# A residual stage of a scan kernel: three quarters of the first pair's output are written to DRAM by rows and copied on later

## The chip, the cores and the metric

The kernel runs on one core of a Trainium2 chip. The time is the device time of one execution in microseconds (us); of several runs the median is given. TensorE (PE) does the matrix products, VectorE (DVE), ScalarE (ACT) and GpSimd (POOL) the elementwise work, and 16 DMA engines move data between DRAM and the on-chip memory (SBUF). In this kernel DMAs are issued from two queues: that of SyncE (SP) and that of ScalarE (ACT).

## The reference

The input x has 32 images, 48 channels, 64 rows, 128 columns, in float32. Two layers are applied, each `x = x + scan(groupnorm(x))`, with 16 groups of 3 channels and no affine part. A scan has four passes over the whole picture, each a recurrence with a 5-tap convolution over all 48 channels:

```python
def step(w, b):
    def f(carry, inp):
        nxt = inp + _conv1d(carry, w, b)
        return (nxt, nxt)
    return f
```

Down and up go over the 64 rows (the carry is a row of 128 columns), then right and left over the 128 columns (the carry is a column of 64 rows). The up pass starts from the last row that down made and takes the down results as input; right and left follow in the same way. So the four passes are strictly one after the other: 2 x 63 row steps, then 2 x 127 column steps, and each step needs the one before it.

## The kernel before

**Groups, pairs, phases.** The 32 images are four groups of eight (`GB = 8`). A row phase takes one group through down and up, 126 steps; a column phase takes two groups, a pair, through right and left, 254 steps. Each layer has four row phases and two column phases, and the 12 phases stand in the tuple `PHASES`, numbered 0 to 11: phases 2 and 6 are the column phases of layer 0, phases 10 and 11 those of layer 1, for the first and the second pair. Phase 11 is the last, directly after phase 10.

**A step.** 48 channels are put on 128 partitions together with eight neighbouring columns (in a row phase) or eight row classes (row modulo 8, in a column phase): 384 = 3 x 128, cut as `PIECES` says. A step is nine products of 128 x 128 by 128 x 128 against band-shaped weights (`PRODUCTS`), and three DVE operations that add bias and input (line 650). Each product shows as two matmul instructions, so 18 to a step.

**SBUF.** `arena` has three slots and a stage of four tiles. A slot holds either half the rows of a group or a quarter of the columns (32 of 128) of a pair. A column phase has four quarters and three slots: quarter 0 is written to DRAM in the course of the right scan (`spill_unit`, `spill`), quarter 3 goes into its slot, and quarter 0 is read back in the left scan. `slots(k)` turns the order of the slots around from phase to phase: phase 11's quarter 0 lies in the slot of phase 10's quarter 2, and its quarter 1 in that of quarter 1.

**Through DRAM.** A group's rows are written out by the up scan (`move_rows` with `to_dram`, to `upa` in layer 0 and `upb` in layer 1) in pieces of 32 floats, 128 bytes, and read back by columns with `load_unit`, six units to a quarter (three partition groups for each of the pair's two groups), in pieces of up to 8 KB.

**The residual.** In a column phase of layer 1 each quarter has six units. `load_residual` brings a unit of the layer's input (`mid`) into one of two tiles, by the ACT queue. `add_permuted` adds it to the result on POOL, eight instructions, and puts the sum into one of two output tiles in the order of images and columns. `store_result` writes this to `out`, in pieces of 32 floats, 128 bytes, which is what a row of a quarter has in `out`; half of its DMAs are issued from SP and half from ACT. Quarters are done in the order 3, 2, 1, 0, as the left scan finishes them. In phase 11 the last quarter is done otherwise (`last_loads`, `last_results`).

**Order.** The kernel is one list of instructions, made before the launch. `scans` gives the steps; `at(t, fn, ...)` puts other work into an agenda at step number t, and `catch_up` writes out what is due before each step. `in_order` ties each engine's instructions into the order in which they were written, DMA queues too: an instruction that waits holds up all that stands behind it on its engine. The numbers t are thus places in each engine's order and not times. Semaphores come from the data dependences. All DMAs, from both queues, use eight semaphores in turn.

**The start.** `first_group` writes out the first group's work: loading, group statistics, permuting rows into pieces (POOL), writing them to `xin`, reading them back as rows (`move_rows`), scaling (`scale_rows`, on ACT), and the first load of the second group (`take_in(1, 0, ...)`, on SP).

The lines that the change touches: the weight tiles at 139, `store_result` at 618, the loads at the start of a column phase at 795 to 800, the residual tiles at 823 to 847, the end of `first_group` at 1035 and the agenda behind it, 1038 to 1042.

Of the kernel before, what the change touches and what calls it, by code (L numbers as in the profile page):

```python
# [29 lines left out]
F32 = mybir.dt.float32  # L30
# [3 lines left out]
C = 48  # L34
# [7 lines left out]
GB = 8  # L42
E8 = 8
FULL = 128
NG = E8 * C // FULL
NQ = 4
# [45 lines left out]
def kernel(  # L92
# [11 lines left out]
    NH = H // E8  # L104
    KQ = NK // NQ
    WQ = W // NQ
# [3 lines left out]
    UNIT = NH * LINE  # L110
# [5 lines left out]
    CHANNEL = H * W * GB  # L116
# [5 lines left out]
    dram = ctx.enter_context(tc.tile_pool(name="dram", bufs=1, space=bass.MemoryType.DRAM))  # L122
# [10 lines left out]
    def const(shape, name):  # L133
        return cpool.tile(shape, F32, tag=name, name=name)
# [1 line left out]
    arena = const([FULL, 3 * SLOT + 4 * UNIT], "arena")  # L136
    slot = [arena[:, i * SLOT : (i + 1) * SLOT] for i in range(3)]
    stage = arena[:, 3 * SLOT :].rearrange("p (i n) -> p i n", i=4)
    wt = {k: const([FULL, NG, NG * FULL], f"w{k}") for k in ("down0", "down1", "right", "left")}
    bd = const([FULL, NG, 2, 3], "bd")  # L140
    mask_sb = const([P, P], "mask_sb")
    maskp = const([P, NG, FULL], "maskp")
# [4 lines left out]
    def kept(name):  # L147
# [13 lines left out]
        dram.tile([2 * NG, FULL, UNIT], F32, tag=f"spill{i}", name=f"spill{i}")  # L161
        for i in range(4)
    ]

    def by_row(t, e, h0, h1):

# [14 lines left out]
    def dma(dst, src, queue=None):  # L181
        (queue or nc.sync).dma_start(dst, src)
# [21 lines left out]
    def pieces(o):  # L204
        return [(e, c0, c1, p0) for e, c0, c1, g, p0 in PIECES if g == o]
# [39 lines left out]
    def scaling(key, layer, g, averages, masks):  # L245


        n = len(masks)
        yield from averages(key)
        mean_p, var_p = averages.result  # L250

        def average(ps, rhs):
            for i in range(n):
                nc.tensor.matmul(ps, masks[i], rhs[:, i], start=i == 0, stop=i == n - 1)

        def expand(ps, rhs):
            for o in range(NG):
                nc.tensor.matmul(ps[:, o], maskp[:, o], rhs, start=True, stop=True)

        def small(name):  # L260
            return stat_tile([FULL, NG, GB], name, key)

        ps = ps_stat.tile([FULL, 2 * NG + 2, GB], F32, tag="ps_stat", name=f"ps_{key}")
        average(ps[0:P, 0], mean_p)
        yield
        mean_c = stat_tile([P, GB], "mean_c", key)
        nc.vector.tensor_copy(mean_c, ps[0:P, 0])
        yield
        expand(ps[:, 1 : 1 + NG], mean_c)
        yield  # L270
        mean = small("mean")
        nc.vector.tensor_copy(mean, ps[:, 1 : 1 + NG])
        at = mean if n > 1 else mean_c.unsqueeze(1)
        np_ = FULL if n > 1 else P
        spare = small("dev")
        dev = spare[0:np_, 0:n]
        nc.vector.tensor_tensor(dev, mean_p, at, ALU.subtract)
        nc.vector.tensor_tensor(dev, dev, dev, ALU.mult)
        nc.vector.tensor_tensor(dev, dev, var_p, ALU.add)
        yield  # L280
        average(ps[0:P, 1 + NG], dev)
        yield
        var_c = stat_tile([P, GB], "var_c", key)
        nc.vector.tensor_copy(var_c, ps[0:P, 1 + NG])
        yield
        expand(ps[:, 2 + NG :], var_c)
        yield
        var = small("var")
        nc.vector.tensor_scalar(var, ps[:, 2 + NG :], GN_EPS, None, ALU.add)

        std = small("std")
        nc.scalar.activation(std, var, AF.Sqrt)
        yield
        yield
        r0 = std
        nc.vector.reciprocal(r0, std)
        t0 = spare
        nc.vector.tensor_tensor(t0, var, r0, ALU.mult)
        nc.vector.tensor_tensor(t0, t0, r0, ALU.mult)
        yield  # L300
        nc.vector.tensor_scalar(t0, t0, -0.5, 1.5, ALU.mult, ALU.add)
        scale, offset = (
            stat_pool.tile(
                [FULL, NG, GB], F32, tag=f"{t}{layer}{g}", name=f"{t}{layer}{g}"
            )
            for t in ("scale", "offset")
        )
        nc.vector.tensor_tensor(scale, r0, t0, ALU.mult)
        nc.vector.scalar_tensor_tensor(offset, mean, -1.0, scale, ALU.mult, ALU.mult)
        coeffs[layer, g] = scale, offset  # L310
# [259 lines left out]
    HH = NH // 2  # L570
# [47 lines left out]
    def store_result(k, j, i, perm):  # L618
# [5 lines left out]
        for a in range(HH):  # L624
            for e, c0, c1, p0 in pieces(o):
                to = nc.sync if a < HH // 2 else nc.scalar
                dma(dst[e, r * HH + a, c0:c1], src[p0 : p0 + c1 - c0, a], to)


    def step(key, weights, b_at, src, inp, dst, whole, part):  # L630

# [88 lines left out]
    def at(t, fn, *args):  # L720
        agenda.append((t, len(agenda), fn, args))

    def spread(t, gen, every):


        def go(t):
            if next(gen, "end") != "end":
                at(t + every, go, t + every)
                agenda.sort(key=lambda a: a[:2])

        at(t, go, t)
# [58 lines left out]
    def plan_cols(k, t0, prev):  # L790
        _, layer, pair = PHASES[k]
        n = 2 * NG
        after = prev == "cols"
        for i in range(n):
            if follows(k) and UNITS[i][1] == 1:
                other = nc.scalar
                at(t0 - 13 + i, load_unit, k, 0, i, 2, NH, 0, E8, other)
                at(t0 - 6 + i / n, load_unit, k, 0, i, 1, 2, 0, E8, other)
                at(t0 - 1.5, load_unit, k, 0, i, 0, 1, E8 // 4, E8, other)
                at(t0, load_unit, k, 0, i, 0, 1, 0, E8 // 4, other)  # L800
                at(t0 + 1.5, load_unit, k, 1, i)
            else:
                early = 30 if after else 46 if k == 2 else 70
                at(t0 - early + 2 * i, load_unit, k, 0, i)
                at(t0 + (3 if after else 0.5 if follows(k) else -24 + 2 * i), load_unit, k, 1, i)
            at(t0 + (38 if after else 8) + 2 * i, load_unit, k, 2, i)
            at(t0 + 33 + 2 * i, spill_unit, k, i, False)
            at(t0 + 50 + 2 * i, load_unit, k, 3, i)
        final = k == len(PHASES) - 1
        left = t0 + W - 1  # L810
        end = left + W - 1
        for i in range(n):
            at(left + 64 + 2 * i, spill_unit, k, i, True)
        units = []
        for n_done, j in enumerate((3, 2, 1, 0)):
            every = 4.5
            if j == 0 and PHASES[k + 1 if not final else k][0] == "rows":
                every = 7
            units += [(left + 34 + 32 * n_done + every * i, j, i) for i in range(n)]
        stats = None  # L820
        if layer == 0:
            stats = ResultStatsV(f"r{2 * pair}"), ResultStatsA(f"r{2 * pair + 1}")
        tiles = [stage[:, i] for i in range(4)]
        nats, perms = (tiles, None) if layer == 0 else (tiles[0:2], tiles[2:4])
        ahead = len(nats)

        for u, (t, j, i) in enumerate(units):
            nat = nats[u % ahead]
            o, half = UNITS[i]
            if u < ahead:  # L830
                at(left + 16, load_residual, k, j, i, nat)
            elif not (final and j == 0):
                at(units[u - ahead][0] + (3 if layer == 0 else 4.9), load_residual, k, j, i, nat)
            if layer == 0:
                at(t, add_residual, k, j, i, nat)
                at(t + 4, keep_result, k, j, i)
                unit = quarter(k, j)[:, half, o]
                if half == 0:
                    for b in range(GB):
                        at(t + 5 + b, stats[0].take, j, o, unit, b)  # L840
                else:
                    at(t + 1, stats[1].take, j, o, unit)
            elif not (final and j == 0):
                perm = perms[u % 2]
                at(t, add_permuted, k, j, i, nat, perm, [nc.gpsimd])
                at(t + 5, store_result, k, j, i, perm)
        if layer == 0:
            t = units[-1][0] + 14
            g = 2 * pair
            spread(t, scaling(f"r{g}", 1, g, stats[0], r_masks), 1)  # L850
            spread(t + 20, scaling(f"r{g + 1}", 1, g + 1, stats[1], r_masks), 1)
        if final:
            at(left + 97, last_loads, k)
            at(end + 4, last_results, k)
# [29 lines left out]
    starts = [0]  # L884
# [11 lines left out]
    nats = [wide_nat(3 * SLOT, 4)]  # L896
# [15 lines left out]
    def first_group():  # L912
# [29 lines left out]
        for b in range(2 * GB):  # L942
            i, b = divmod(b, GB)
# [88 lines left out]
        scale_rows(0, 24, 32)  # L1032
        move_rows(0, 32, 48, False)
        scale_rows(0, 32, 40)
        move_rows(0, 48, 56, False)
        take_in(1, 0, nats1[0])

    in_order(first_group)
    at(starts[0] + 10, scale_rows, 0, 40, 48)
    at(starts[0] + 20, move_rows, 0, 56, 64, False)  # L1040
    at(starts[0] + 22, take_in, 1, 16, nats1[1])
    at(starts[0] + 34, scale_rows, 0, 48, 64)

    agenda.sort(key=lambda a: a[:2])
    done = 0
# [65 lines left out]
```

## Time and profile before

| | |
|---|---|
| median of 3 runs | 4545.84 us (4545.33 to 4550.96) |
| the profiled execution | 4548.13 us, span of its instructions 4546.3 us |
| mean granted clock of TensorE | 0.964 |
| busy share of the span: PE, DVE, ACT, POOL | 92%, 48%, 26%, 20% |
| DMA: packets, bytes | 2,124,132, 661.55 MB; 2,010,816 packets under 512 B |
| DMA: mean rate | 146 GB/s |

Phases in the span, by the names of the step tiles: phase 0 from about 140 us, phase 1 from 410, phase 2 (`step_00r`, `step_00l`) from 677, phase 6 (`step_01r`, `step_01l`) from 1995, phase 10 (`step_10r`, `step_10l`) from 3303, phase 11 (`step_11r`, `step_11l`) from 3814 to 4422. A name such as `step_11r` reads: layer 1, pair 1, right; `step_00d` is layer 0, group 0, down. The rest of the span, to 4546, is output.

How to read it: a view of waits gives, for an engine and an operation, what it waited for and for how long, in total, how often, and the longest. Where it names an operation that had long been done, the wait was for another one that ended at the same time, often a DMA. A view by stretches gives the busy time of each engine in a window, the granted clock (1.00 is full speed), the share of the 16 DMA engines and the rate. Every instruction of the residual addition has line 614, every DMA line 182, every product of a step line 641.

### The profile page before, as it was taken

Reading aid. Unit: us, or ns where it says so; the run is one execution under the profiler, and the core shown is the slowest. Engines: PE = TensorE matmul, PEld = TensorE weight load, DVE = VectorE, ACT = ScalarE, POOL = GpSimd, SP = SyncE. Lnnn points to the kernel's source line nnn. Section 1 sums busy time; section 2 is a strip of 40 time slices with the busy share of each in tenths; the row PEclk is TensorE's granted clock in tenths of the full one; section 3 lists DMA queues with packets and bytes.
Section 4 is the critical chain, followed back from the end, with each engine's and each line's share of the span. In section 5 each row is a group of like instructions: output and inputs, shape, how many; then the busy total and the mean of one; then the engine's idle time right before and its main releaser. Section 6 shows DMA issues by size and latency. Waiting matters only on the chain.

```text
span 4546.3 us, 90798 instructions
## 1 busy us (share of the span) xinstructions
PE 4163.2 (92%) x36632; PEld 4132.1 (91%) x36632; DVE 2180.9 (48%) x6594; ACT 1183.5 (26%) x2334; POOL 907.7 (20%) x943
## 2 busy tenths in 40 slices
PE   4889997999999999979999999999999997879990
PEld 2889997999999999979999999999999997869990
DVE  5445443446654444434456654444444443334441
ACT  1553302426776445000025944330000000000000
POOL 4441001314412020000024300000000155500554
PEclk9999998999999999989999999999999998889995
DMA  9989789857989999489038989394790099970799
GB/s 176 176 163 157 114 146 194 202 105 237 221 163 160 162 150 155 75 151 199 6 89 241 204 148 150 48 143 84 117 207 12 18 195 181 200 188 1 148 172 163
DMA packets 2124132, 661.55 MB, mean 146 GB/s; under 512 B 2010816, under 2 KB 2063808, under 8 KB 2092224
## 3 DMA queue, kind: packets, MB, share of 16 engines
q1 hardware_dynamic: 1901312, 573.92, 66.5%
q10 hardware_dynamic: 222400, 81.83, 9.5%
q8 instruction: 288, 4.72, 0.5%
q14 instruction: 132, 1.08, 0.1%
HBM read 378.70 MB, written 277.11 MB: 144 GB/s over the span
## 4 chain that ended last, share of the span: by engine, by line
PE 77%; DMA 15%; SPq 2%; ACT 2%; POOL 1%; ACTq 1%; issue 1%; DVE 0%; POOLq 0%; DVEq 0%
DMA out<-arena 6%; PE step_01r L641 6%; PE step_00r L641 6%; PE step_10r L641 6%; PE step_00l L641 6%; PE step_01l L641 6%; DMA arena<-mid 4%; PE step_11r L641 3%; PE step_00u L641 3%; PE step_11d L641 3%; PE step_02u L641 3%; PE step_11u L641 3%; PE step_10u L641 3%; PE step_13u L641 3%; PE step_13d L641 3%; PE step_12u L641 3%
## 5 line engine op out<-in xcount | busy, mean ns | idle before, releaser
L525 ACT ACTIVATE arena<-arena,offset,scale 128x256 f32<-128x256 f32 (+2 forms) x840 | 594.7, 802 | 449.3 <-DVE arena L650 151.8
L614 POOL TENSOR_TENSOR arena<-arena 128x256 f32<-128x256 f32 x336 | 349.1, 1082 | 973.1 <-DVE arena L650 717.6
L482 POOL COPY arena<-arena 112x256 f32<-112x256 f32 x458 | 270.9, 648 | 764.1 <-DMA arena<-in_x 469.0
L880 ACT COPY arena<-arena 128x256 f32<-128x256 f32 x18 | 10.5, 644 | 1470.9 <-DMA out<-arena 1467.9
L594 POOL TENSOR_TENSOR arena<-arena 128x2048 f32<-128x2048 f32 x48 | 217.7, 4562 | 835.7 <-PE step_01l L641 543.5
L641 PE MATMUL step_11r<-arena,wright 128*128 128x128 f32 x2286 | 267.3, 281 | 85.7 <-DVE arena L650 37.6
L641 PEld LDWEIGHTS step_11r<-arena,wright 128*128 128x128 f32 x2286 | 265.4, 198 | 87.5 <-DVE arena L650 55.8
L416 ACT ACTIVATE junk<-arena 128x256 f32<-128x256 f32 x192 | 129.6, 675 | 699.2 <-POOL arena L594 693.1
L641 PE MATMUL step_01r<-arena,wright 128*128 128x128 f32 x2286 | 258.8, 277 | 29.3 <-DMA arena<-upa 29.3
L641 PEld LDWEIGHTS step_01r<-arena,wright 128*128 128x128 f32 x2286 | 258.4, 194 | 29.7 <-issue 29.5
L641 PE MATMUL step_00r<-arena,wright 128*128 128x128 f32 x2286 | 257.4, 276 | 29.2 <-DMA arena<-upa 29.2
L641 PEld LDWEIGHTS step_00r<-arena,wright 128*128 128x128 f32 x2286 | 257.0, 193 | 29.6 <-issue 29.4
L641 PE MATMUL step_00l<-arena,wleft 128*128 128x128 f32 x2286 | 256.3, 275 | 0.0
L641 PE MATMUL step_10r<-arena,wright 128*128 128x128 f32 x2286 | 256.0, 275 | 0.0
L641 PEld LDWEIGHTS step_10r<-arena,wright 128*128 128x128 f32 x2286 | 255.7, 192 | 0.3
L641 PEld LDWEIGHTS step_00l<-arena,wleft 128*128 128x128 f32 x2286 | 255.7, 192 | 0.0
L641 PE MATMUL step_01l<-arena,wleft 128*128 128x128 f32 x2286 | 255.4, 275 | 0.0
L641 PE MATMUL step_10l<-arena,wleft 128*128 128x128 f32 x2286 | 255.4, 275 | 0.0
L641 PE MATMUL step_11l<-arena,wleft 128*128 128x128 f32 x2286 | 255.4, 275 | 0.0
L641 PEld LDWEIGHTS step_01l<-arena,wleft 128*128 128x128 f32 x2286 | 255.3, 192 | 0.0
L641 PEld LDWEIGHTS step_10l<-arena,wleft 128*128 128x128 f32 x2286 | 255.3, 192 | 0.0
L641 PEld LDWEIGHTS step_11l<-arena,wleft 128*128 128x128 f32 x2286 | 255.3, 192 | 0.0
(173 smaller groups left out, 6989.0 us busy)
## 6 DMA issues: line engine op xcount, KB each, us to landing
xin<-arena SPq DMA_DIRECT2D x96, 384.0 KB, 5.5
arena<-xin SPq DMA_DIRECT2D x96, 384.0 KB, 8.5
mid<-arena SPq DMA_DIRECT2D x96, 384.0 KB, 8.0
arena<-mid SPq DMA_DIRECT2D x192, 192.0 KB, 4.4
upb<-arena SPq DMA_DIRECT2D x192, 192.0 KB, 3.9
arena<-mid ACTq DMA_DIRECT2D x192, 192.0 KB, 4.7
arena<-upb SPq DMA_DIRECT2D x96, 384.0 KB, 10.7
arena<-xin SPq DMA_DIRECT2D x186, 192.0 KB, 4.3
```

The source lines that it names most:

```text
L416: nc.scalar.activation(junk[:, 0:n], view[:, b], AF.Identity, accum_out=self.sum[:, i, j : j + 1])
L482: copy(dst[:, r, q], src[:, r0 + r, q])
L525: nc.scalar.activation(args[0], args[0], AF.Identity, bias=args[2], scale=args[1])
L594: nc.gpsimd.tensor_tensor(unit, unit, nat, ALU.add)
L614: engines[(2 * a + s) % len(engines)].tensor_tensor(dst[:, a, s], res[:, a, s], inp[:, a, s], ALU.add)
L641: nc.tensor.matmul(part(whole(ps[o]), -s), weights[:, i, FULL * (o - NG * s - i + 1) : FULL * (o - NG * s - i + 2)], part(src(i), s), star ...
L880: copy(dst[:, a, s], src[:, a, s])
```

## The change

Five edits:

1. In phase 10, quarters 2, 1 and 0 are no longer written to `out` by `store_result`. `hold_result` writes a unit's sums to a tensor in DRAM, `held[j]`, which has channels, rows, images and the 32 columns of the quarter, in that order; a piece is a row with all its 16 images, 512 floats, 2 KB. One DMA for each entry of `PIECES`, from SP. Quarter 3 goes to `out` as before.
2. In the agenda of phase 11, from step 63 on, 96 DMAs from SP copy from `held` to `out`, each for one image and 24 channels: 1536 pieces of 128 bytes, 192 KB, DRAM to DRAM.
3. In layer 1 the residuals have a third tile, and their loads stand one unit earlier in the order. The tile is the first 2048 of the 2304 columns of `downs`, a tile that joins the weights `down0` and `down1`.
4. In phases 2 and 6, which follow the row phase of their second group, the first quarter's load for that group is cut once more: rows 32 to 63 at 31 steps before the phase, rows 16 to 31 at 13 steps before it, where rows 16 to 63 were.
5. In the first group, rows 56 to 63 are read with rows 48 to 55 in `first_group`, ahead of the first load of the second group, and not at step 20; rows 48 to 55 and 56 to 63 are scaled apart, at steps 26 and 32, and not together at 34.

```diff
@@ -136,7 +136,9 @@
     arena = const([FULL, 3 * SLOT + 4 * UNIT], "arena")
     slot = [arena[:, i * SLOT : (i + 1) * SLOT] for i in range(3)]
     stage = arena[:, 3 * SLOT :].rearrange("p (i n) -> p i n", i=4)
-    wt = {k: const([FULL, NG, NG * FULL], f"w{k}") for k in ("down0", "down1", "right", "left")}
+    wt = {k: const([FULL, NG, NG * FULL], f"w{k}") for k in ("right", "left")}
+    downs = const([FULL, 2, NG, NG * FULL], "downs")
+    wt |= {f"down{i}": downs[:, i] for i in range(2)}
     bd = const([FULL, NG, 2, 3], "bd")
     mask_sb = const([P, P], "mask_sb")
     maskp = const([P, NG, FULL], "maskp")
@@ -161,6 +163,11 @@
         dram.tile([2 * NG, FULL, UNIT], F32, tag=f"spill{i}", name=f"spill{i}")
         for i in range(4)
     ]
+
+    HELD = (2, 1, 0)
+    held = {
+        j: dram.tile([C, 2 * CHANNEL // NQ], F32, tag=f"held{j}", name=f"held{j}") for j in HELD
+    }
 
     def by_row(t, e, h0, h1):
 
@@ -626,6 +633,19 @@
                 to = nc.sync if a < HH // 2 else nc.scalar
                 dma(dst[e, r * HH + a, c0:c1], src[p0 : p0 + c1 - c0, a], to)
 
+    def hold_result(j, i, perm):
+        o, r = divmod(i, 2)
+        n = 2 * GB * WQ
+        dst = held[j].rearrange("c (a e n) -> e c a n", e=E8, n=n)[:, :, r * HH : (r + 1) * HH]
+        for e, c0, c1, p0 in pieces(o):
+            dma(dst[e, c0:c1], perm[p0 : p0 + c1 - c0].rearrange("p (a n) -> p a n", n=n))
+
+    def let_result(j, b, part):
+
+        src = held[j][part].rearrange("c (h b n) -> b (c h) n", b=2 * GB, n=WQ)
+        dst = out[b, part].rearrange("c h w -> (c h) w")
+        dma(dst[:, j * WQ : (j + 1) * WQ], src[b])
+
 
     def step(key, weights, b_at, src, inp, dst, whole, part):
 
@@ -794,7 +814,8 @@
         for i in range(n):
             if follows(k) and UNITS[i][1] == 1:
                 other = nc.scalar
-                at(t0 - 13 + i, load_unit, k, 0, i, 2, NH, 0, E8, other)
+                at(t0 - 31 + i, load_unit, k, 0, i, 4, NH, 0, E8, other)
+                at(t0 - 13 + i, load_unit, k, 0, i, 2, 4, 0, E8, other)
                 at(t0 - 6 + i / n, load_unit, k, 0, i, 1, 2, 0, E8, other)
                 at(t0 - 1.5, load_unit, k, 0, i, 0, 1, E8 // 4, E8, other)
                 at(t0, load_unit, k, 0, i, 0, 1, 0, E8 // 4, other)
@@ -822,6 +843,8 @@
             stats = ResultStatsV(f"r{2 * pair}"), ResultStatsA(f"r{2 * pair + 1}")
         tiles = [stage[:, i] for i in range(4)]
         nats, perms = (tiles, None) if layer == 0 else (tiles[0:2], tiles[2:4])
+        if layer:
+            nats.append(downs.rearrange("p i g n -> p (i g n)")[:, 0:UNIT])
         ahead = len(nats)
 
         for u, (t, j, i) in enumerate(units):
@@ -843,12 +866,20 @@
             elif not (final and j == 0):
                 perm = perms[u % 2]
                 at(t, add_permuted, k, j, i, nat, perm, [nc.gpsimd])
-                at(t + 5, store_result, k, j, i, perm)
+                if final or j not in held:
+                    at(t + 5, store_result, k, j, i, perm)
+                else:
+                    at(t + 5, hold_result, j, i, perm)
         if layer == 0:
             t = units[-1][0] + 14
             g = 2 * pair
             spread(t, scaling(f"r{g}", 1, g, stats[0], r_masks), 1)
             spread(t + 20, scaling(f"r{g + 1}", 1, g + 1, stats[1], r_masks), 1)
+        if layer and not final:
+            for n in range(len(HELD) * 4 * GB):
+                n_done, i = divmod(n, 4 * GB)
+                part = slice(i % 2 * C // 2, (i % 2 + 1) * C // 2)
+                at(end + 63 + 0.95 * n, let_result, HELD[n_done], i // 2, part)
         if final:
             at(left + 97, last_loads, k)
             at(end + 4, last_results, k)
@@ -1032,14 +1063,14 @@
         scale_rows(0, 24, 32)
         move_rows(0, 32, 48, False)
         scale_rows(0, 32, 40)
-        move_rows(0, 48, 56, False)
+        move_rows(0, 48, 64, False)
         take_in(1, 0, nats1[0])
 
     in_order(first_group)
     at(starts[0] + 10, scale_rows, 0, 40, 48)
-    at(starts[0] + 20, move_rows, 0, 56, 64, False)
     at(starts[0] + 22, take_in, 1, 16, nats1[1])
-    at(starts[0] + 34, scale_rows, 0, 48, 64)
+    at(starts[0] + 26, scale_rows, 0, 48, 56)
+    at(starts[0] + 32, scale_rows, 0, 56, 64)
 
     agenda.sort(key=lambda a: a[:2])
     done = 0
```

## The prediction, made before the changed kernel ran

> **What bounds the kernel now.** I read the page first: the product engine is busy 92% of the span, so only the places where it stands still can be won. Then the list of its waits, which gives those places, and then the busy times by stretch, cut at the phase borders.
>
> ```profile
> span 4546.3 us, 90798 instructions
> PE 4163.2 (92%) x36632; PEld 4132.1 (91%) x36632; DVE 2180.9 (48%) x6594; ACT 1183.5 (26%) x2334; POOL 907.7 (20%) x943
> ```
>
> ```profile
> PE rows L970 <- DMA arena<-in_x: 45.0, 1, 45.0
> PE step_11r L641 <- DVE arena L650: 37.6, 4, 18.8
> PE step_00d L641 <- DVE arena L650: 34.8, 3, 19.2
> PE step_11r L641 <- DMA arena<-mid: 32.8, 2, 16.9
> PE step_01r L641 <- DMA arena<-upa: 29.3, 1, 29.3
> PE step_00r L641 <- DMA arena<-upa: 29.2, 1, 29.2
> PE step_11r L641 <- DMA arena<-upb: 15.3, 1, 15.3
> ```
>
> (Engine, operation, what it waited for: total us, times, longest.) The three rows of `step_11r`, the last right scan, hold 37.6+32.8+15.3 = 85.7 us: the largest stop after the start. The two `upa` rows are the starts of the first two column phases.
>
> ```profile
> 3682.00:3814.00 132.00, 132.00 (x1185) 132.00 (x1184) 62.98 (x198) 0.00 (x0) 65.96 (x65) 1.00 0.98 198
> 3814.00:4055.00 241.00, 155.32 (x1288) 153.60 (x1288) 69.31 (x215) 0.00 (x0) 85.93 (x83) 0.80 1.07 214
> 4055.00:4225.00 170.00, 170.00 (x1523) 169.93 (x1523) 81.21 (x254) 0.00 (x0) 0.00 (x0) 1.00 0.05 11
> 4225.00:4420.00 195.00, 195.00 (x1749) 195.00 (x1748) 93.13 (x292) 0.00 (x0) 116.64 (x112) 1.00 0.89 174
> 4420.00:4546.00 126.00, 2.43 (x22) 2.24 (x21) 24.56 (x23) 10.47 (x18) 49.36 (x50) 0.52 1.03 166
> 2670.00:2796.00 126.00, 126.00 (x1132) 126.00 (x1131) 62.82 (x210) 66.28 (x90) 0.00 (x0) 1.00 1.02 147
> ```
>
> (Stretch, length, busy us of PE, its weight loads, DVE, ACT, POOL; then granted clock, DMA share, GB/s.) From 3682 to 4055 the DMA engines are full, and in the second stretch PE works 155 of 241 us, at clock 0.80. It does 1288/18 = 71.6 steps there; a step at full clock is 2.01 us (63 steps of `step_12d` take 126.63), so 144 us would do: 97 us are lost, 86 idle and 11 to the lower clock. Then 170 us follow with the DMA engines at 5%, and then the end, where they are full again and PE has been done since 4422. So the loss is a queue of transfers before an empty stretch.
>
> ```profile
> POOL arena L614 <- DMA arena<-mid: 73.6, 11, 20.5
> POOL arena L614 <- DMA out<-arena: 44.7, 17, 11.4
> POOL arena L614 <- DMA arena<-upb: 29.9, 3, 11.9
> ```
>
> (GpSimd's waits, 3600 to 3980.) The first pair's 24 additions of the residual need 200 us and take 356: 148 us pass waiting for transfers. They free the slots into which the last phase loads its quarters, so each late addition becomes a late load.
>
> **The change, part by part.** *Results held.* 18 of 24 units of phase 10 (quarters 2, 1, 0) no longer go out in 128-byte pieces. Removed are 18 x 13.3 = 240 DMAs, half on SP and half on ACT, with 18 x 8192 = 147,456 pieces. In the stretch 2670 to 2796, where all transfers are 128-byte pieces, 147 GB/s at a share of 1.02 make 14.2 ns a piece and engine: 147,456 x 14.2 / 16 = 131 us of all DMA engines. Added are 60 DMAs on SP alone with 9216 pieces of 2 KB. No such store is in the trace; its packet records have 46 ns for a 1 KB store and 309 for 8 KB, so 77 to 92 ns, I take 85: 49 us. Saved: 82 us of a full queue. ACT then issues only residual loads in these quarters, and no longer stands behind an addition before it can issue the next one. Behind a held store on SP, which waits for POOL's addition, stand the spill and the quarter loads of phase 11, as behind the old stores. All DMAs share eight semaphores in turn, so fewer DMAs also block each other less.
>
> The Trainium skill ("DMA: Bandwidth & Descriptors", "Latency and other measured facts") speaks against this store: row pitches that are large powers of two lose bandwidth, 207 GB/s at 512 KiB and 103 at 4 MiB, and padding restores it. The held tensor has a bare pitch of 128 KiB a channel where the neighbouring tensors are padded; at 103 GB/s the 18.9 MB would cost an estimated 183 us and the gain would turn into a loss. No row here shows that pitch.
>
> *What it buys.* Unless noted, the last right scan would start at 3814 as now. Its quarters are due at 3814, +32 steps = 3878, +64 = 3942, +96 = 4006. From about 3690 the additions can run at their written pace, 9.05 us a unit (4.5 steps) against 8.7 us of POOL work (8 x 1.08): quarter 2 ends near 3750, quarter 1 near 3815 to 3835, quarter 0 near 3880 to 3895. The DMA work due by 3878, by packet records: 16 residual units at 4.25 us (256 packets of 265 ns) = 68, 17 held units at 2.7 = 46, the spilled quarter back 19 (768 at 400), two quarters loaded 29 each (768 at 600): 191 us against 188. So quarters 0 and 1 come about in time. Quarter 2 can load after 3885: spill 15, itself 29, three early residuals of phase 11 13 = 57 us, done near 3942. I leave 10 us of the 97 standing: gain 87, bounds 55 (an over-full queue and two stops left) and 97.
>
> *Passing on.* 96 DMAs on SP, 147,456 pieces, DRAM to DRAM. They wait for held stores alone; SP order puts them behind the quarter-3 loads, so they run from about 3965. Behind them on SP stand only phase 11's outputs, on ACT its residual loads (through the shared semaphores), needed from 3814+255+68 = 4137. Free are 172-13 = 159 us. The trace has no long copy of this kind; its few DRAM-to-DRAM packets (192 B, `taps` from `in_w`) have a median of 15 ns in light traffic, 26 in the crowded start. Bounds: 14.2 (read and write overlap) and 28.4 (they add): 131 to 262 us. I take 15, the nearest row: 138 us, inside 159, cost 0. If the cover goes, every us beyond it delays the full queue of the end, less some 20 us of gaps there. The issues themselves (0.4 to 0.6 us each on SP in the trace, 96 make some 50) fit too.
>
> *Third residual tile.* It removes waits for `mid`, but the two output tiles stay, and waits for stores follow: the end's full queue (0.89, then 1.03) leaves about 15 us. I take 4, bounds 0 and 15. It lies in weight storage last used in phase 9. The merged weight tile costs nothing if dependences go by region, as in `arena`; if not, one weight load (about 15 us) would stop phase 3.
>
> *Rows 32 to 63 loaded earlier at two column starts.* 2/3 of a 2.36 MB load (8 us each time) leaves the last 26 us before the border. DMA share there is 0.52 to 0.72 earlier on and 1.16 later, so it fits. But the chain that ends the stop is store, load, store, load of the last eight rows, and it begins only when row 2 is done. I take 2.5 each of 29: 5, bounds 0 and 16. The ACT queue has nothing else there.
>
> *First group.* Rows 56 to 63 are loaded before the second group's first take-in, not between its two; scaling splits in two. That ends the 19.2 us stop at 227. But the next phase's rows wait for POOL's permutes of the second group, which end at 362.2 by a chain of transfers that PE's pace does not set; the 10 DMAs (10.8 us) now stand before that group instead. Most comes back as a stop at the next border: gain 2, bounds -5 and 10.
>
> Sum: 87+4+5+2 = 98. The profiled execution took 4548.1 (span 4546.3), which makes 4450; the median of the runs is 2.3 lower: 4448.
>
> **Rivals.** *Slower: the copies are dear.* From 3965 a copy at x ns a piece takes 9216x ns. It decides at 159 + 20 + 98 = 277 us, 30 ns a piece; at 45 ns, 415 us, the end comes 138 us after today's: about 4685. For it: read and write both in DRAM, no long row. Against: the 15 ns row, and loads and stores of 128 B each sustain 14.2. *Stops form again:* held stores at 2 x 85 ns add 49 us, or SP's order makes quarters 1 and 2 late; half the gain stays, 4495. *No change:* additions were the pace all along. Against: 24 x 8.7 = 208 us from 3621 end at 3829, not 3977; 4546. *Better:* upper bounds of the small parts, 97+15+16+10: about 4410.
>
> **How the numbers follow.** Forecast 0.60 (its own range 4430 to 4470), stops again 0.20 (4470 to 4530), better 0.06, no change 0.02, slower 0.12 (4556 to 4750). The range 4420 to 4525 leaves out the slower case and the edges. A measurement tells 0.2%, 9 us, from no change; faster 0.86, same 0.02, slower 0.12.
>
> **What would show it.** The `step_11r` rows should fall from 85.7 to under 20 us with clock near 1; waits of POOL for `out` and `mid` should halve. The copies should fill part of the empty stretch and be over before phase 11's first addition; if share 1 runs on into the end and PE-end to span-end grows beyond 125 us, the copy price was wrong. The `upa` waits should be some 27 each, the 19.2 gone, a new wait in `step_01d`.

## The result, and the profile after

The changed kernel takes 4553.43 us (median of 12 runs, 4548.91 to 4558.82) against 4549.59 for the kernel before (12 runs): a ratio of 1.0009, 95% interval 1.0000 to 1.0018. That is no change. The forecast was 4448.

The page of the changed kernel:

```profile
span 4551.0 us, 90606 instructions
PE 4164.5 (92%) x36632; PEld 4133.9 (91%) x36632; DVE 2182.1 (48%) x6594; ACT 1190.0 (26%) x2358; POOL 906.5 (20%) x943
```

PE's waits in it (engine, operation, what it waited for: total us, times, longest):

```profile
PE step_11r L661 <- DVE arena L670: 30.6, 3, 12.1
PE step_10r L661 <- DVE arena L670: 27.0, 2, 18.0
PE step_00r L661 <- DMA arena<-upa: 26.7, 1, 26.7
PE step_11r L661 <- DMA arena<-upb: 26.3, 3, 15.1
PE step_01r L661 <- DMA arena<-upa: 24.5, 1, 24.5
PE step_00d L661 <- DVE arena L670: 20.6, 3, 10.9
PE step_10r L661 <- DMA arena<-upb: 11.5, 1, 11.5
PE step_00u L661 <- DVE arena L670: 9.5, 1, 9.5
```

The last right scan, `step_11r`, waits 56.9 us where it waited 85.7: less, but not the 10 of the forecast. And the right scan of phase 10, `step_10r`, which had no wait before, has two rows, 38.5 us in all. Nothing in the change was meant to touch that scan.

PE's order of time around it (start, length, engine, what ran; in brackets the idle time before):

```profile
3294.06 1.14 PE L661 MATMUL step_10r<-arena,wright 128*128 128x128 f32 x8
3306.68 65.44 PE L661 MATMUL step_10r<-arena,wright 128*128 128x112 f32 x570 [11.48 <-DMA arena<-upb]
3381.15 1.65 PE L661 MATMUL step_10r<-arena,wright 128*128 128x128 f32 x6 [9.04 <-DVE arena L670]
3400.78 192.92 PE L661 MATMUL step_10r<-arena,wright 128*128 128x112 f32 x1702 [17.98 <-DVE arena L670]
...
3848.80 1.06 PE L661 MATMUL step_11r<-arena,wright 128*128 128x128 f32 x8
...
4170.55 255.44 PE L661 MATMUL step_11l<-arena,wleft 128*128 128x128 f32 x2286
```

The starts of the same scans in the kernel before:

```profile
3303.03 256.05 PE L641 MATMUL step_10r<-arena,wright 128*128 128x128 f32 x2286
3814.18 0.61 PE L641 MATMUL step_11r<-arena,wright 128*128 128x128 f32 x4
4167.00 255.43 PE L641 MATMUL step_11l<-arena,wleft 128*128 128x128 f32 x2286
```

With these the books close:

| stretch | before | after | difference |
|---|---|---|---|
| to the start of phase 10 | 3303.0 | 3294.1 | -9.0 |
| phase 10 | 511.2 | 554.7 | +43.6 |
| right scan of phase 11 | 352.8 | 321.8 | -31.1 |
| left scan of phase 11 | 255.4 | 255.4 | 0 |
| from the end of PE to the end | 123.9 | 125.0 | +1.1 |

The sum is +4.6; the spans differ by 4.7 us. So the change did gain 40 us, and a new stop of 44 us took them.

SP's queue, phase 9 and after (the length of a row is the time from its first issue to its last), first two rows of the kernel before, then the changed kernel:

```profile
3086.87 24.62 SPq L182 DMA_DIRECT2D arena<-upb  x20
3190.18 74.05 SPq L182 DMA_DIRECT2D upb<-arena  x50
```

```profile
3078.51 220.98 SPq L189 DMA_DIRECT2D arena<-upb  x20
3299.86 55.19 SPq L189 DMA_DIRECT2D upb<-arena  x50
3355.14 13.86 SPq L189 DMA_DIRECT2D arena<-upb  x14
3369.66 17.02 SPq L189 DMA_DIRECT2D upb<-arena  x10
```

ACT's queue in the changed kernel (3100 to 3660):

```profile
3294.03 3.14 ACTq L189 DMA_DIRECT2D downs<-mid  x7
```

And what SP waited for (3100 to 3420):

```profile
SPq L189 <- DMA downs<-mid: 195.4, 4, 193.9
SPq L189 <- DMA arena<-upb: 13.9, 10, 3.8
```

Issuing the twenty loads of phase 10's first quarters took 25 us before and takes 221 now: seventeen are issued by 3104, the last three not before 3297.8. SP waits 194 us in one piece for a load into `downs`, the third residual tile. ACT issues seven of the eight loads into `downs` at 3294, when phase 9's last products have read the weights there. Behind SP's blocked load stand the 80 stores of phase 9's rows to `upb`, which before began at 3190 and now begin at 3300, and behind these phase 10's loads.

The stretches of the changed kernel (length, busy us of PE, its weight loads, DVE, ACT, POOL, then clock, DMA share, GB/s):

```profile
3660.00:3849.00 189.00, 189.00 (x1695) 189.00 (x1694) 90.23 (x282) 0.00 (x0) 119.98 (x116) 1.00 0.90 206
3849.00:4060.00 211.00, 154.09 (x1298) 152.76 (x1297) 69.78 (x216) 0.00 (x0) 74.61 (x72) 0.85 0.90 227
4060.00:4191.00 131.00, 131.00 (x1175) 130.93 (x1174) 62.65 (x196) 0.00 (x0) 0.00 (x0) 1.00 0.98 155
4426.00:4551.00 125.00, 0.00 (x0) 0.00 (x0) 23.51 (x19) 10.44 (x18) 49.53 (x51) 0.51 1.02 164
```

In the right scan of phase 11 PE still stops, but the DMA engines are no longer full throughout: a share of 0.90 where it was 1.07 (3849 to 4060 in both). The copies from `held` to `out` fill 4060 to 4191, the stretch that was empty, and the part after PE is no longer than it was. GpSimd's waits in the first pair's additions (3640 to 4000), without the wait for the scan itself:

```profile
POOL arena L621 <- DMA held<-arena: 88.9, 4, 40.8
POOL arena L621 <- DMA out<-arena: 31.3, 4, 12.7
POOL arena L621 <- DMA arena<-mid: 11.7, 3, 8.9
```

The waits for residuals (`mid`) fell from 73.6 to 11.7, those for `out` from 44.7 to 31.3, and a new one came, 88.9 us for the held stores: an output tile is not free until its store has landed. In SP's queue one sees why it lands late:

```profile
3798.10 28.57 SPq L189 DMA_DIRECT2D arena<-upb  x10
3827.24 4.36 SPq L189 DMA_DIRECT2D held<-arena  x3
3834.82 18.73 SPq L189 DMA_DIRECT2D arena<-upb  x10
3856.61 42.26 SPq L189 DMA_DIRECT2D held<-arena  x17
3901.84 35.81 SPq L189 DMA_DIRECT2D arena<-upb  x20
3940.00 54.91 SPq L189 DMA_DIRECT2D held<-arena  x20
...
4060.54 130.41 SPq L189 DMA_DIRECT2D out<-held  x96
```

The held stores of quarters 1 and 0 stand behind the loads of phase 11's first two quarters. While SP works off 20 loads (3901.84 to 3937.65), POOL comes to stand with both output tiles full (40.8 us, from 3912.6 on), and with POOL stand the additions that free the slots for the next loads. The DMA engines are busy with these loads (share 1.03 from 3913 to 3940) and have room before and after (0.78 from 3868 to 3913, 0.74 from 3940 to 3960).

### The profile page after: what moved, and what is told of

Same layout as the page of the kernel before. It is cut to its first block, busy times and chain, and to the rows that moved or that the text cites. A ratio compares the mean times of both kernels' runs of the same rounds, so it can differ in the third digit from the quotient of the medians.

```text
span 4551.0 us, 90606 instructions
## 1 busy us (share of the span) xinstructions
PE 4164.5 (92%) x36632; PEld 4133.9 (91%) x36632; DVE 2182.1 (48%) x6594; ACT 1190.0 (26%) x2358; POOL 906.5 (20%) x943
## 3 DMA queue, kind: packets, MB, share of 16 engines
q14 instruction: 131, 1.07, 0.1%
## 4 chain that ended last, share of the span: by engine, by line
PE 83%; DMA 9%; POOL 2%; SPq 2%; ACT 1%; issue 1%; ACTq 1%; DVE 1%; POOLq 0%; DVEq 0%
PE step_00r L661 6%; PE step_01r L661 6%; PE step_00l L661 6%; PE step_01l L661 6%; PE step_10r L661 6%; PE step_11l L661 6%; PE step_11r L661 4%; PE step_10l L661 3%; PE step_02u L661 3%; PE step_11d L661 3%; PE step_11u L661 3%; PE step_10u L661 3%; PE step_13u L661 3%; PE step_13d L661 3%; PE step_12u L661 3%; PE step_12d L661 3%
## 5 line engine op out<-in xcount | busy, mean ns | idle before, releaser
L621 POOL TENSOR_TENSOR arena<-arena 128x256 f32<-128x256 f32 x224 | 232.7, 1082 | 830.7 <-DVE arena L670 733.0
L661 PE MATMUL step_11r<-arena,wright 128*128 128x128 f32 x2286 | 265.0, 280 | 56.9 <-DVE arena L670 30.6
L661 PE MATMUL step_10r<-arena,wright 128*128 128x128 f32 x2286 | 261.1, 278 | 38.5 <-DVE arena L670 27.0
L661 PE MATMUL step_01r<-arena,wright 128*128 128x128 f32 x2286 | 257.3, 276 | 24.5 <-DMA arena<-upa 24.5
L661 PE MATMUL step_11l<-arena,wleft 128*128 128x128 f32 x2286 | 255.4, 275 | 0.0
L661 PE MATMUL step_01l<-arena,wleft 128*128 128x128 f32 x2286 | 255.4, 275 | 0.0
L661 PE MATMUL step_10l<-arena,wleft 128*128 128x128 f32 x2286 | 255.4, 275 | 0.0
L661 PEld LDWEIGHTS step_11l<-arena,wleft 128*128 128x128 f32 x2286 | 255.4, 192 | 0.0
```

The costliest lines, as they stand in the source:

```text
L621: engines[(2 * a + s) % len(engines)].tensor_tensor(dst[:, a, s], res[:, a, s], inp[:, a, s], ALU.add)
L661: nc.tensor.matmul(part(whole(ps[o]), -s), weights[:, i, FULL * (o - NG * s - i + 1) : FULL * (o - NG * s - i + 2)], part(src(i), s), star ...
```

## Experiments

Theory A is that the third tile's first load makes the new stop in phase 10, through the semaphores that both queues share. For the right scan of phase 11, theory C is that the held stores' place on SP keeps the additions late, and theory D that the DMA engines' work does.

### The change without its third tile, and the third tile alone

```diff
 # e1: the changed kernel, without
-        if layer:
-            nats.append(downs.rearrange("p i g n -> p (i g n)")[:, 0:UNIT])
 # e2: the kernel before, with the merged weight tile `downs` and
+        if layer:
+            nats.append(downs.rearrange("p i g n -> p (i g n)")[:, 0:UNIT])
```

> The changed kernel without its third residual tile, the rest as changed. Theory A (the load into the weight storage waits for phase 9 and, through the shared semaphores, holds SP for 194 us): the waits of step_10r (38.5 us) and the 194 us wait of SP go, phase 11 starts at 3804 to 3808, the time falls by 40 to 45 us to about 4510. Theory B (the late start of phase 10 has another cause, such as the held tensors or the earlier loads): step_10r waits stay, time 4545 to 4565. If the third tile also earned something in phases 10 and 11, waits of POOL for mid come back and part of the 40 is lost: 4520 to 4535.

> The kernel before with the third residual tile alone. Theory A: a wait of SP of about 190 us on the load into downs and 35 to 45 us of step_10r waits appear, and the time rises by 30 to 45 us, to 4580 to 4595. Theory B: within 10 us of before.

Without the tile: 4522.0 us against 4557.2 for the kernel before on that chip, ratio 0.9925 (0.9908 to 0.9943). No `step_10r` wait is left, phase 11 starts at 3807.9, and POOL's waits for `mid` are back at 25.0 us, from 11.7. The tile alone, put into the kernel before: 4607.6 us, ratio 1.0112 (1.0096 to 1.0127), 50 us slower, more than the 30 to 45 expected; phase 10 takes 556.7 us there, 45.5 more than before. SP's waits in that kernel (3040 to 3420):

```profile
SPq L184 <- DMA downs<-mid: 192.7, 4, 190.9
SPq L184 <- DMA arena<-upb: 30.6, 18, 4.7
```

and PE's:

```profile
PE step_10r L643 <- DVE arena L652: 28.4, 2, 17.8
PE step_10r L643 <- DMA arena<-upb: 12.3, 1, 12.3
```

The tile makes the stop, with the other edits and without them. Theory B falls.

### The same tile, its first load from SP

```diff
+        def first(u):
+            return [nc.sync] if layer and not final and u == 2 else []
-                at(left + 16, load_residual, k, j, i, nat)
+                at(left + 16, load_residual, k, j, i, nat, *first(u))
```

(`load_residual` takes the queue as an argument; all other residual loads stay on ACT.)

> The changed kernel, all three tiles, but the first load into the weight storage is issued from SP, where it stands behind the loads of phase 10, and not from ACT. Theory A: step_10r waits under 5 us, phase 11 starts at 3804 to 3808, time 4500 to 4512; the tile itself is harmless, only where its first load stands. Theory B: as the changed kernel, 4553.

4515.5 us, just above the range of theory A, ratio 0.9911 (0.9893 to 0.9928). `step_10r` has no wait, phase 11 starts at 3808.8, and in SP's list of waits (3040 to 3420) 0.3 us are left for `downs`. So not the storage is at fault, only where the load stands: on ACT nothing is ahead of it, so it is at the head of its queue already in phase 9, it has its turn on the semaphores, and SP's later DMAs on these wait for it. The changed kernel's trace shows it: SP's first blocked load, issued at 3297.76, waits for the semaphore numbered 107, which had been given ahead of it to a load into `downs`; that one is issued at 3294.37 and lands at 3297.75, and the two have no data in common. Issued from SP, it stands behind phase 10's first loads (its eight DMAs are issued from 3399 on) and holds up none of them.

Whether the third tile earns anything stays open: 4515.5 with it and 4522.0 without, and the intervals of the two ratios overlap. In the kernel before it earned nothing in the last scan: with the tile alone `step_11r` waits 88.6 us (85.7 before), and POOL's waits for `mid` fall to 1.0 us while those for `out` rise to 141.2 (3600 to 4000).

### Held stores from ACT

```diff
-            dma(dst[e, c0:c1], perm[p0 : p0 + c1 - c0].rearrange("p (a n) -> p a n", n=n))
+            dma(dst[e, c0:c1], perm[p0 : p0 + c1 - c0].rearrange("p (a n) -> p a n", n=n), nc.scalar)
```

> As the kernel with the first load from SP, and the held results are stored from ACT and not from SP. Theory C (in phase 11 POOL waits 89 us for held stores that stand on SP behind the quarter loads, and this, not the DMA engines' work, leaves 57 us of step_11r waits): POOL's waits for held fall below 25 us, step_11r waits below 25, time 4465 to 4485. Theory D (the DMA engines are the bound there, the order on SP does not matter): step_11r waits stay at 50 to 60 us and the time within 8 us of the kernel with the first load from SP.

4497.2 us, ratio 0.9870 (0.9853 to 0.9886), 18 us below the one before it on the same chip, with intervals apart. `step_11r` waits 35.7 us, where 54.3 were left. The size is missed (25 at most was expected). POOL's waits (3640 to 4060) tell why:

```profile
POOL arena L621 <- DMA arena<-mid: 73.2, 5, 17.1
POOL arena L621 <- DMA held<-arena: 44.1, 6, 16.3
POOL arena L621 <- DMA out<-arena: 31.5, 8, 9.9
```

The wait for the stores falls from 60.1 us to 44.1, and that for residuals is back, 73.2 from 3.4: on ACT the held stores wait for additions, and residual loads now stand behind them. The first quarter of phase 11 comes in time, the second 7.5 us late and the third 28.2. The place in the queue matters, but moving all the stores moves the wait too.

### The two small edits alone

```diff
-                at(t0 - 13 + i, load_unit, k, 0, i, 2, NH, 0, E8, other)
+                at(t0 - 31 + i, load_unit, k, 0, i, 4, NH, 0, E8, other)
+                at(t0 - 13 + i, load_unit, k, 0, i, 2, 4, 0, E8, other)
-        move_rows(0, 48, 56, False)
+        move_rows(0, 48, 64, False)
-    at(starts[0] + 20, move_rows, 0, 56, 64, False)
-    at(starts[0] + 34, scale_rows, 0, 48, 64)
+    at(starts[0] + 26, scale_rows, 0, 48, 56)
+    at(starts[0] + 32, scale_rows, 0, 56, 64)
```

> The kernel before with the two small edits alone: rows 32 to 63 loaded earlier in phases 2 and 6, and the first group's rows 56 to 63 read earlier. In the changed kernel phase 10 starts 9 us sooner than before. If these edits bring that, phase 10 starts 5 to 9 us sooner here, the upa waits are 24 to 28 us, and the time is 3 to 10 us less than before. If it is scatter between executions: within 3 us of before.

4538.9 us against 4547.8, ratio 0.9981 (0.9972 to 0.9990): some 9 us (4.5 to 12.7 by the interval). Phase 10 starts at 3294.9, 8 us sooner, and the `upa` waits are 25.7 and 23.7. A single start of phase 10 says less than the ratio: in the ten profiled kernels with these two edits it lies between 3291.3 and 3303.3, in the two without them at 3303.0 and 3308.3.

### Nothing held, and a quarter of the bytes

```diff
 # e6, on the kernel with the first load from SP
-                    at(t + 5, hold_result, j, i, perm)
-                at(end + 63 + 0.95 * n, let_result, HELD[n_done], i // 2, part)
 # e10, on the same: one row in four, and no copies
-        ...[:, :, r * HH : (r + 1) * HH]
+        ...[:, :, r * HH : r * HH + 1]
-            ... perm[p0 : p0 + c1 - c0].rearrange(...)
+            ... perm[p0 : p0 + c1 - c0, 0:n].rearrange(...)
-                at(end + 63 + 0.95 * n, let_result, HELD[n_done], i // 2, part)
```

> The kernel with the first load from SP; quarters 2, 1 and 0 of the first pair are neither held nor copied on, so that part of the output is missing. It takes away the stores' share of the DMA engines and the additions' wait for them. Theory C (the held stores behind SP's loads stop the additions): POOL's 60 us of waits for held go, step_11r waits fall from 54 to under 15 us, time under 4475. Theory D (loads and residuals alone fill the DMA engines): step_11r waits stay above 30 us. The empty stretch before the outputs of phase 11 comes back; if the copies cost nothing the part from the end of PE to the end stays at 124 to 127 us.

> The kernel with the first load from SP, with all 60 held stores issued from SP at their places, each of one row in four (a quarter of the bytes, 12 to 16 us of DMA time and not 64), and without the copies; so that part of the output is missing. With the stores it has 54 us of step_11r waits, without them 13. Theory C (the stores' place in SP's order, behind the quarter loads, holds the additions up): POOL's waits for held stay at 40 us or more and step_11r waits at 35 to 54. Theory D (it is the stores' DMA time): the waits fall to 13 to 25 us.

Without stores and copies the time is 4455.8 us (one run, as for the next kernel), and `step_11r` waits 13.2 us:

```profile
PE step_11r L661 <- DVE arena L670: 9.8, 1, 9.8
PE step_11r L661 <- DMA arena<-upb: 3.4, 1, 3.4
```

So the held stores are behind most of the 54 us; the copies can't be, since with them SP issues the first at 4022, and the last stop ends at 4000. The part after PE is 124.6 us here (4329.5 to 4454.1), and 125.9 in the kernel with stores and copies that it was made from: the copies cost nothing there.

With 60 stores of a quarter of the bytes the time is 4483.1 us. PE's wait:

```profile
PE step_11r L661 <- DVE arena L670: 29.8, 3, 13.7
```

and of POOL's waits (3600 to 4000) this one:

```profile
POOL arena L621 <- DMA held<-arena: 25.9, 2, 18.1
```

Full bytes 54.3, a quarter 29.8, none 13.2. The packet records give the stores 62.6 us of DMA time with full bytes and 16.2 with a quarter. So, taken in this order and from one execution each, the bytes account for 24.5 us of PE's waits, and the stores as such, their number and place, for 16.6. Neither theory alone gives these numbers: C asked for 35 to 54, D for 13 to 25. Both causes are at work, and the 13 us are left to the loads, the residuals and quarter 3. One more is not taken apart by any run: the semaphores that both queues share. In the changed kernel SP waits 27.8 us from 3890 to 3960 for residual loads of ACT (20.6 for `arena<-mid`, 7.2 for `downs<-mid`), with which its own DMAs there share only the turn.

### All four quarters held, and three with both queues

```diff
 # e7: as with held stores from ACT, and
-    HELD = (2, 1, 0)
+    HELD = (3, 2, 1, 0)
-                at(end + 63 + 0.95 * n, let_result, HELD[n_done], i // 2, part)
+                at(end + 63 + 0.74 * n, let_result, HELD[n_done], i // 2, part)
 # e8: as e7, and the stores from
+            ... nc.sync if j > 1 else nc.scalar
 # e9: as e8, but HELD = (2, 1, 0) and 0.95 as in the change
```

> As the kernel with held stores from ACT, but quarter 3 is held too, and 128 copies run instead of 96. Quarter 3 then costs about 21 us of DMA time and 20 DMAs in place of 43 us and 80. If DMA work and the number of DMAs are what is left, the additions of quarter 3 run at 8.7 us a unit and not 12, step_11r waits fall from 36 to 10 to 25 us, time 4475 to 4488. If 128 copies (174 us) run into the outputs of phase 11, the part from the end of PE to the end grows by 5 to 15 us and the time stays at 4490 to 4500.

> As the one with all quarters held, but quarters 3 and 2 are stored from SP, where no quarter loads stand before them, and quarters 1 and 0 from ACT. If the residual loads on ACT are held up by held stores that wait for the addition (POOL waits 73 us for mid with all held stores on ACT), those waits halve and the time is 5 to 15 us below the kernel with all held from ACT. If the DMA engines are the bound, no difference (within 5 us).

> The kernel with three quarters held, quarter 2 stored from SP and quarters 1 and 0 from ACT, 96 copies as in the change. With all four quarters held this order left 19 us of step_11r waits, but 128 copies made the part after PE 130 us and not 113 to 114. If both parts add as seen, the waits here are 20 to 36 us, the part after PE is 113 to 116 us, and the time is 4470 to 4485, at or below the best so far. If the order of the stores gained only together with quarter 3's smaller work, the waits are 36 us or more and the time is that of the kernel with held stores from ACT, 4495.

(The last expectation counts the end of PE on the trace's own clock, some 11 us ahead of the span's; by the spans its 130 us are 141.5, and its 113 to 114 are 124 to 125.)

| | right scan of phase 11 | `step_11r` waits | part after PE | time | ratio |
|---|---|---|---|---|---|
| three held, ACT | 297.9 | 35.7 | 126.8 | 4497.2 | 0.9870 (0.9853 to 0.9886) |
| four held, ACT | 289.6 | 28.5 | 138.0 | 4494.3 | 0.9884 (0.9869 to 0.9898) |
| four held, both queues | 277.1 | 18.6 | 141.5 | 4482.4 | 0.9854 (0.9838 to 0.9871) |
| three held, both queues | 290.5 | 30.4 | 123.7 | 4475.4 | 0.9838 (0.9825 to 0.9852) |

With four quarters held from ACT the waits miss the 10 to 25 expected; the time is the one given for copies that run into the outputs. The order is worth 10 us of waits at four quarters and 5 at three. With four quarters it brings the time forecast, 12 us less, but not by the waits that were named: POOL's waits for `mid` only go from 38.9 to 35.5 us (3600 to 4000), and those for the held stores from 49.7 to 8.5. Quarter 3's copies run past the end of the empty stretch: SP's rows for the copies in the two kernels with both queues, first with four quarters held,

```profile
3989.95 176.94 SPq L189 DMA_DIRECT2D out<-held  x128
4166.99 51.91 SPq L189 DMA_DIRECT2D out<-arena  x40
```

then with three,

```profile
4001.76 131.63 SPq L189 DMA_DIRECT2D out<-held  x96
4157.24 56.72 SPq L189 DMA_DIRECT2D out<-arena  x40
```

Three end 24 us before phase 11's first outputs, four run straight into them, and what quarter 3 saves in the scan (8 and 13 us) is given back at the end (11 and 18 us). Three held, with quarter 2 from SP and quarters 1 and 0 from ACT, has the lowest time of the whole kernels here, 1.6% below the one before; from the version with four, run on another chip, it is not told apart by the intervals.

## Why the prediction was wrong, step by step

**Where the 103 us went.** The sum was 98 us of gain, and the profiled execution is 4.7 us slower. The third tile accounts for 48 of the difference (4 forecast, a loss of 44), the last right scan for 56 (87 forecast, 31 measured); the other terms held within 2 us each.

**The third residual tile is the step that failed outright.** The prediction took 4 us of gain (0 to 15) and asked only whether its storage was free and whether the merged weights would tie dependences together. They did not: phase 3 has no stop of the 15 us that were feared (7.5 us in one place, 4.6 before). But the load's issue was not followed. The prediction knew that the eight semaphores go round both queues and counted it as a gain of fewer DMAs alone. It did not ask when ACT reaches this load, which is phase 9, and who comes after it in the semaphores' turn, which is SP with phase 10's loads and, behind these, phase 9's stores. The cost was 44 us in phase 10 here, 50 us by itself. It lay outside every range and no rival had it.

**"Quarters 0 and 1 come about in time" was mis-sized: 87 us forecast, 31 measured, 32 with the third tile mended.** The sum counted DMA work against deadlines. The work itself fell nearly as forecast: 2 KB stores have a median of 84 ns and a mean of 111, 64 us for all against 49; the 128-byte pieces removed took 135 against 131; so 71 us were saved, not 82. But the additions did not run at their written pace. The prediction named what stands behind a held store on SP; it did not name what the held store stands behind. With quarter loads ahead of it the output tiles stay full (POOL waits 88.9 us), and the share of the DMA engines falls to 0.90 in the stretch that was to be bound by them. All three quarters came late, with stops of 15, 19 and 23 us. Changing the order alone (54.3 to 35.7 with ACT, 30.4 with both queues) and changing the bytes (29.8) each take a third to under a half of the waits. (A unit of additions is priced once at 200/24 = 8.3 us and once at 8.7; the time that 192 of POOL's instructions cover in the trace, 199.6 us, gives 8.3. Nothing hangs on it.)

**The copies: right.** Forecast 138 us and no cost; measured 131 us (4060 to 4191) and 1 us. That is the lower bound of the sum, 14.2 ns a piece; the packet records have a mean of 13.2. Only their start was 95 us later than forecast, since everything ahead of them was; the empty stretch was late too. The slower rival's mechanism, copies that run into the end, is real, but from a larger amount: 128 copies make the last part 11 to 18 us longer.

**Early rows at the column starts, first group: right.** Forecast 5 and 2 us, together 7; phase 10 starts 9 us sooner, and alone they give 9, with an interval of 4.5 to 12.7. The `upa` stops fell by 2.5 and 4.8. The 19.2 us stop of the first group went, and most of it came back as expected, though elsewhere: 9.5 us in `step_00u`, where DVE waits for the next group's rows for its statistics, and not in `step_01d` as forecast; phase 1 starts 3.5 us sooner.

**The row-pitch rule did not bind.** The prediction weighed a rule of the Trainium skill ("DMA: Bandwidth & Descriptors", "Latency and other measured facts") against the rows. That page's figures are for copies of tiles with 16 KiB a partition between tensors in DRAM, at pitches from 512 KiB up, and its full rate is 214 GB/s. So its 207 at 512 KiB is hardly a loss, and the prediction's estimate took the figure for 4 MiB. Here, at a pitch of 128 KiB, unpadded, the 2 KB stores took 84 ns in the median and 111 in the mean, on 16 engines 390 and 295 GB/s; the estimate of 183 us stands against 64 measured. No run pads the tensor, so what padding would bring is not shown.

**The chances.** "Stops form again" had 0.20 with half the gain; it came true at a third of the gain, and the third tile took the rest. That the time ended at no change is a coincidence of a gain of 40 us and a loss of 44. "No change" had 0.02, for a reason (the additions' pace) that is not what happened.

## What to carry to other kernels

A DMA that comes to its turn before it can run holds up what stands behind it: for every moved or new DMA, ask when its queue reaches it, and which other queue has to come after it on a shared semaphore. Where a queue carries both stores that free a buffer and loads that wait for that buffer's next use, sum the DMA work, but also write out the order: a store behind 20 loads is late by the time that SP takes to issue them, here 36 us. Bundled edits can cancel: take the stretches apart by phase before judging any of them, as a result of "no change" here hid 40 us of gain, and 74 us with the order mended.

## What the runs showed of the hardware that was not expected

Copies from DRAM to DRAM in 128-byte pieces ran as fast as stores from SBUF: 96 of 192 KB in 131 us is 144 GB/s, against 147 where only 128-byte loads and stores ran (2670 to 2796 in the kernel before); the packet records have a mean of 13.2 ns a piece against 14.1. That both sides lie in DRAM did not show.

The eight DMA semaphores tie the two queues together over long times: a residual load that was not ready held up unrelated loads, and the stores behind them, on the other queue for 194 us, while the DMA engines stood at a share of 0.04 (3100 to 3294; 0.51 in the kernel before).
